# Small tiles shared, odd maxima searched a step ahead, and small maps written in halves, in a two-layer convolution and attention kernel

## The chip, the cores and the metric

The kernel runs on one core of a Trainium2 chip. The metric is the device time of one execution in microseconds (us). The engines are TensorE (PE, with its weight loads shown apart as PEld), VectorE (DVE), ScalarE (ACT), GpSimd (POOL) and SyncE (SP), which here only issues DMAs. All data are 32-bit floats.

## The reference

The input x has 8 images of 256 channels and 64 x 64 pixels. Two layers follow each other, each added to its input after a group norm `_gn` over 32 groups of channels.

```python
# layer 0, on n = _gn(x)
x1, x2, x3 = conv1x1(n, w1, b1), conv1x1(n, w2, b2), conv1x1(n, w3, b3)   # 32, 32, 256 maps
h = relu(bn1(concat([x1, unfold3(pad(x2, "reflect"))])))                  # 32 + 9 * 32 maps
w = conv1x1(relu(bn2(conv1x1(h, cw1))), cw2, cb2)      # 9 weights for each of 32 groups
x = x + einsum("bgskhw,bgkhw->bgshw", unfold3(pad(x3)), w)

# layer 1, on n = _gn(x)
q, k, v = conv1x1(n, Wq, bq) * HD**-0.5, conv1x1(n, Wk, bk), conv1x1(n, Wv, bv)   # 4 heads of 64
att = softmax(q . (unfold7(pad(k, "reflect")) + unfold7(pad(pe, "reflect"))))     # 49 neighbours
out_att = sum over neighbours of att * unfold7(pad(v, "reflect"))
wts = softmax over 9 of conv1x1(n, Wfc)                # 9 maps for each channel
out_conv = sum over 9 of depthwise(relu(depthwise(n, w1)), w2) * wts
x = x + rate1 * out_att + rate2 * out_conv
```

## The kernel before

An image is cut into 8 bands of 8 rows. The main loop runs over g from -12 to 63. For g at or above 0 it does layer 1 of band i = g % 8 of image b = g // 8, and beside it layer 0 of the band that lies 12 ahead (AHEAD), so layer 0 ends at g = 51. For g below 0 only layer 0 runs ("alone"). A band has 8 steps: s = 0 to 3 for the first 128 channels, 4 to 7 for the others. m = s % 4 is the step within a half, and a step covers two tiles of 8 x 8 queries. An image's first and last bands (i = 0 and 7) have another order of queries and keys than the six between.

The order of the work is the order in which Python issues it: each engine runs its instructions in that order. A step consists of fixed parts with six calls of `advance()` between them. `after(n, f)` puts f off by n such calls (six are one step), so that an instruction is issued when its operands should be there. `beside(g, s)` returns three lists of extra work for a step: `head` (issued before the exponentials), `mid` (in the middle) and `end`. `steer(g, s)` issues loads and starts the statistics. What a function in `mid` returns is called one `advance()` later.

PSUM has eight banks here: four with the tag "gen", two for scores ("sco"), one "small", one "acc". "gen" serves the results of most matmuls: `pf` (branch weights, L883), `p3` (value maps of layer 0, L373; the trace calls them p), `pq` and `pk` (queries L681, keys L703), `pv` (values, L598), `ptp` (transposed probabilities, L784), `pw` (tap weights, L468), and the group means `pg` (L242), biases `pb` (L308) and channel means `pgc` (L546). A bank is handed on when the instruction that reads it has run: ACT's exponential L888 for pf, its copies L786, L378 and L605 for ptp, p3 and pv, DVE's products L481 for pw.

The "small" bank has one buffer, a new one for each even step. It holds the weighted values of two steps (256 columns, matmuls L796, added to xr by DVE at L815), and in part of the steps, beside them, the small maps of layer 0 (p12, columns 256 to 511 at s = 0, L332) or the 32 hidden maps (columns 256 to 383 at s = 4 and 6, L432).

A step in layer 1: at even m, PE makes the scores of two steps (L747) and the weighted values of earlier ones. `masked` (DVE, L761) searches the maxima of one step, `exponentials` (ACT, L769) follows, `probabilities` takes a reciprocal on DVE (L776) and scales on ACT (L778). `branch_weights` runs twice a step: four matmuls into pf and an exponential into ex; POOL adds ex (L1099). `depthwise_begin` and `depthwise_middle` give taps on DVE (L840, L866), two at a time. `keys` ends in four DVE instructions a piece (L711, L718) that write the key block kb with its mirrored columns. `dynamic_sum` divides by the sum of the exponentials (L896 to L910, with DVE's reciprocals L904).

Layer 0 beside it: `small_maps` (four matmuls, each in several instructions) and `write_maps`, eight ACT copies (L347, L351) into x2 and four POOL copies for its edges (L355 to L364); `value_maps`; `hidden_maps` (ACT L422); `tap_weights` with products on DVE (L481) that POOL adds to xg (L489).

Statistics: `gn_affine` runs a1 to a6, spread by `after`: two group means on PE (k = 0 and 1), DVE arithmetic between (a2 reads the first, L251 to L255; a4 the second, L263), ACT for the root (L146), DVE for the biases (L273). It is used by `scaled_weights` (at i = 3 for the next image of layer 0, ending in `through` and `biases`, L316) and by `norm_rows` (at i = 6 for the next image of layer 1, ending in `by_channel` and `take`, L551), both from step 2.

Values: `values` makes them in two halves, ACT copies them to vc (L605), `store_values` writes vc to DRAM (L618, L622), `mirror_rows` mirrors rows there (L629), `value_tile` loads them as vt (L640). `position` makes the position term pe on POOL for the first image and keeps it in DRAM (L661, on SP's queue). Those that `beside` moves:

```python
if s == 3 and not early:
    mid.append(lambda: keys(b, i, 1))
...
made = [(b + 1, 0, (3, 4)), (b + 1, 1, (5, 7))]
...
if s in d and (j < NB or s == d[0]):
    mid.append(lambda bb=bb, j=j, d=d: values(bb, j, d.index(s)))
if s == d[1]:
    end.append(lambda bb=bb, j=j: store_values(bb, j))
```

Of the kernel before, what the change touches and what calls it, by code (L numbers as in the profile page):

```python
# [10 lines left out]
F32 = mybir.dt.float32  # L11
# [7 lines left out]
P = 128  # L19
C = 256  # L20
NCT = C // P
H = W = 64
HW = H * W
R = 8
# [63 lines left out]
def conv_layers_kernel(ctx: ExitStack, tc: tile.TileContext, ins: dict, out: bass.AP):  # L88
# [131 lines left out]
    def after(n, f):  # L220
        later.append((place[0] + n, f))

    def advance():
# [3 lines left out]
        for f in ready:  # L227
            f()

    def gn_affine(sts, means, name, done):  # L230


        n = len(sts)
        mv = stat.tile([P, n, 2], F32, name=f"mv_{name}", tag=f"mv{n}")
        for ct, st in enumerate(sts):
            nc.vector.bn_aggr(mv[:, ct, :], st)
        mean, var = mv[:, :, 0], mv[:, :, 1]
        gm, d, sc, bi = (stat.tile([P, n], F32, name=f"{v}_{name}", tag=f"{v}{n}") for v in ("gm", "d", "sc", "bi"))

        def group_means(v, k):  # L240
            pg = ps.tile([P, n], F32, name=f"pg_{name}_{k}", tag="gen", bufs=4)
            nc.tensor.matmul(pg, means, v, start=True, stop=True)  # L242
            return pg


        def a1():
            pg = group_means(mean, 0)
            after(2, lambda: a2(pg))

        def a2(pg):  # L250
            nc.vector.tensor_copy(gm, pg)  # L251
            for ct in range(n):
                c = slice(ct, ct + 1)
                nc.vector.tensor_scalar(d[:, c], pg[:, c], mean[:, c], None, ALU.subtract)
                nc.vector.tensor_scalar(d[:, c], d[:, c], d[:, c], var[:, c], ALU.mult, ALU.add)  # L255
            after(5, a3)

        def a3():
            pg = group_means(d, 1)
            after(2, lambda: a4(pg))  # L260

        def a4(pg):
            nc.vector.tensor_scalar(sc, pg, GN_EPS, None, ALU.add)  # L263
            after(2, a5)

        def a5():
            inverse_root(sc)
            after(4, a6)

        def a6():  # L270
            for ct in range(n):
                c = slice(ct, ct + 1)
                nc.vector.tensor_scalar(bi[:, c], gm[:, c], sc[:, c], -1.0, ALU.mult, ALU.mult)  # L273
            done(sc, bi)

        after(3, a1)
# [15 lines left out]
    def scaled_weights(b):  # L292

        im = images[b]

        def scale(sc, bi):
            im.w12s = w0.tile([P, NCT, 2 * REL], F32, tag="w12s", name=f"w12s_{b}", bufs=1)
            im.w3s = w0.tile([P, NCT, C], F32, tag="w3s", name=f"w3s_{b}", bufs=1)
            for kt in range(NCT):
                nc.scalar.activation(im.w12s[:, kt], w12[:, kt], AF.Copy, scale=sc[:, kt : kt + 1])  # L300
                nc.scalar.activation(im.w3s[:, kt], w3[:, kt], AF.Copy, scale=sc[:, kt : kt + 1])
            after(5, lambda: through(bi))

        def through(bi):
            pb = ps.tile([P, 1 + NCT], F32, tag="gen", name=f"pb_{b}", bufs=4)
            for m, to, w in ((0, 0, w12), (0, 64, w12), (1, 0, w3[:, :, :P]), (2, 0, w3[:, :, P:])):
                for kt in range(NCT):
                    nc.tensor.matmul(  # L308
                        pb[to : to + w.shape[2], m : m + 1], w[:, kt], bi[:, kt : kt + 1],
                        start=(kt == 0), stop=(kt == NCT - 1),  # L310
                    )
            after(2, lambda: biases(pb))

        def biases(pb):
            im.bias = w0.tile([P, 1 + NCT], F32, tag="bias", name=f"bias_{b}")
            nc.vector.tensor_add(im.bias[:, 0:1], pb[:, 0:1], par[:, PB21 : PB21 + 1])  # L316
            for ct in range(NCT):
                nc.vector.tensor_add(
                    im.bias[:, 1 + ct : 2 + ct], pb[:, 1 + ct : 2 + ct], chan[:, ct, CB3 : CB3 + 1]
                )  # L320

        gn_affine([im.st0[:, ct] for ct in range(NCT)], gmat, f"a{b}", scale)

    def small_maps(b, i, home):


        im = images[b]

        p12 = home[:, 2 * P :].rearrange("p (r c) -> p r c", r=R // 2)
        for kt in range(NCT):  # L330
            for u in range(2):
                nc.tensor.matmul(  # L332
                    p12[64 * u : 64 * u + 64], im.w12s[:, kt, :],
                    im.xc[i][:, kt, u * BAND // 2 : (u + 1) * BAND // 2],
                    start=(kt == 0), stop=(kt == NCT - 1),
                )
        return lambda: write_maps(b, i, p12)

    def write_maps(b, i, p12):
        im = images[b]  # L340
        t = im.x2[i] = w0.tile([P, HR, W], F32, tag="x2", name=f"x2_{b}_{i}", bufs=2)
        bias = im.bias
        for u in range(2):
            r, o = u * R // 2, 64 * u
            for q, (dst, src) in enumerate(((1, 0), (0, 0), (0, 1))):
                n = W - (q != 1)
                nc.scalar.activation(  # L347
                    t[32 * q : 32 * q + 32, r + 1 : r + 1 + R // 2, dst : dst + n],
                    p12[o : o + 32, :, src : src + n], AF.Identity, bias=bias[o : o + 32, 0:1],
                )  # L350
            nc.scalar.activation(  # L351
                t[96:128, r : r + R // 2, :], p12[o + 32 : o + 64], AF.Identity, bias=bias[o + 32 : o + 64, 0:1]
            )

        nc.gpsimd.tensor_copy(t[0:32, 1 : 1 + R, 0:1], t[0:32, 1 : 1 + R, 2:3])  # L355
        nc.gpsimd.tensor_copy(t[64:96, 1 : 1 + R, W - 1 : W], t[64:96, 1 : 1 + R, W - 3 : W - 2])

        if i == 0:
            nc.gpsimd.tensor_copy(t[0:96, 0, :], t[0:96, 2, :])
        else:  # L360
            nc.gpsimd.tensor_copy(t[0:96, 0, :], im.x2[i - 1][0:96, R, :])
            nc.gpsimd.tensor_copy(im.x2[i - 1][0:96, R + 1, :], t[0:96, 1, :])
        if i == NB - 1:
            nc.gpsimd.tensor_copy(t[0:96, R + 1, :], t[0:96, R - 1, :])  # L364
# [168 lines left out]
    def norm_rows(b):  # L533
# [7 lines left out]
            after(3, lambda: by_channel(both))  # L541

        def by_channel(both):
            pg = ps.tile([P, NCT, 2], F32, tag="gen", name=f"pgc_{b}", bufs=4)
            for ct in range(NCT):
                nc.tensor.matmul(pg[:, ct], gc[:, ct], both, start=True, stop=True)  # L546
            after(2, lambda: take(pg))
# [35 lines left out]
    def values(b, j, half):  # L583
# [2 lines left out]

        im = images[b]
        if half == 0:
            im.vc[j] = w1.tile([P, R // 2, C], F32, tag="vc", name=f"vc_{b}_{j}", bufs=1)
        vc, yp = im.vc[j], im.yp[min(j, NB - 1)]  # L590
        first, last, _ = value_rows(j)
        pv = ps.tile([P, 2, C], F32, tag="gen", name=f"pv_{b}_{j}_{half}", bufs=4)
# [54 lines left out]
    def position(b, i):  # L647
# [10 lines left out]
            perow[:, a : a + n].unsqueeze(2).to_broadcast([P, n, W]),  # L658
        )
        kept[i] = dram.tile([P, n, W], F32, tag=f"pe{i}", name=f"pe_{i}", bufs=1)  # L660
        nc.sync.dma_start(out=kept[i], in_=pe[:, :n])  # L661

    kept = {}

# [259 lines left out]
    def beside(g, s):  # L924
# [6 lines left out]
        if g >= 0:  # L931
            if s == 2:
                mid.append(lambda: keys(b, i, 1) if early else queries(b, i, 1))
            if s == 3 and early:
                head.append(lambda: queries(b, i, 1))
            if s == 3 and not early:
                mid.append(lambda: keys(b, i, 1))
        edge = inx in (0, NB - 1)
        if 0 <= g + 1 < B * NB:
            if s == 5 - edge:  # L940
# [5 lines left out]

        made = [(b, i + 2, (4, 5))] if g >= 0 and i < NB - 1 else []
        if i == NB - 1 and 0 <= b + 1 < B:
            made = [(b + 1, 0, (3, 4)), (b + 1, 1, (5, 7))]
        for bb, j, d in made:  # L950
            if s in d and (j < NB or s == d[0]):
                mid.append(lambda bb=bb, j=j, d=d: values(bb, j, d.index(s)))
# [21 lines left out]
        if 0 <= g + AHEAD < B * NB:  # L974
            bq_, iq = divmod(g + AHEAD, NB)
            if alone and s == 0:
                mid.append(lambda: small_maps(bq_, iq, small_tile(f"{bq_}_{iq}"))())
            if s == (2 if alone else 0):
                (mid if alone else end).append(lambda: value_maps(bq_, iq, 0, alone))
            if s == (3 if alone else 1):  # L980
# [40 lines left out]
    with tc.manual_schedule():  # L1021
# [17 lines left out]
        for n, f in enumerate(layer1_loads()):  # L1039
            after(4 * STEPS * (3 + n), f)  # L1040

        pending, before, conv, convs = [], None, None, []
        for g in range(-AHEAD, B * NB):
            b, i = divmod(g, NB)
            for s in range(STEPS):
                ct, m = divmod(s, NT // 2)
                head, mid, end = beside(g, s)
                steer(g, s)
                if g >= 0:
                    nm = f"{b}_{i}_{ct}_{m}"  # L1050
                    weighted = []
                    if m % 2 == 0:
                        sco = score_tile(nm)
                        for e in range(2):
                            scores(b, i, ct, m + e, sco)
                        small = small_tile(nm)
                        weighted, pending = weigh_steps(pending, small), []
                        if s == 0 and g + AHEAD < B * NB:
                            mid.append(small_maps(*divmod(g + AHEAD, NB), small))
                        if s in (4, 6) and convs:  # L1060
                            convs.pop()(small)
                        if before is not None:
                            pending.append((before[:-1], transposed(nm, before[-1])))
                    prob, nmax = masked(nm, m, sco)
                    for a, po in weighted:
                        add_values(*a, po)
                ahead = [f() for f in head]
# [41 lines left out]
                advance()  # L1109
                for f in end:  # L1110
                    f()
                advance()
        for last in (before, None):
            for a, po in weigh_steps(pending, small_tile(f"end{last is None}")):
# [88 lines left out]
```

## Time and profile before

| What | Before |
|---|---|
| median of 3 runs | 3902.41 us (3900.53 to 3902.47) |
| profiled execution | 3901.4 us |
| its span | 3899.5 us |
| PE, DVE, ACT, POOL busy | 97%, 88%, 72%, 80% of the span |
| layer 0 alone, up to band 0's scores | 233.5 us |
| a band between two starts of scores, i = 1, 2, 4, 5 | 57.5 to 57.6 us in most |
| the same, i = 3, 6, 7, 0 | 60.4, 57.5, 61.2, 59.5 us in most |
| bands without layer 0 (g = 56 to 62) | 47.2 to 49.6 us |

The span runs from the first instruction of the program to the last; the execution's own time is 1.9 us longer. A timeline row gives start and length in us, engine, line, operation, what is written and read, a count of merged instructions, and in brackets the idle time before and who ended it. A row of waits gives who waited for whom, the total in us, how often, and the longest. The granted PE clock was 0.994 of full over the span, and 1.00 in every stretch that I read from 300 us to 3800 us.

### The profile page before, as it was taken

Reading aid. Unit: us, or ns where it says so; the run is one execution under the profiler, and the core shown is the slowest. Engines: PE = TensorE matmul, PEld = TensorE weight load, DVE = VectorE, ACT = ScalarE, POOL = GpSimd, SP = SyncE. Lnnn points to the kernel's source line nnn. Section 1 sums busy time; section 2 is a strip of 40 time slices with the busy share of each in tenths; the row PEclk is TensorE's granted clock in tenths of the full one; section 3 lists DMA queues with packets and bytes.
Section 4 is the critical chain, followed back from the end, with each engine's and each line's share of the span. In section 5 each row is a group of like instructions: output and inputs, shape, how many; then the busy total and the mean of one; then the engine's idle time right before and its main releaser. Section 6 shows DMA issues by size and latency. Waiting matters only on the chain.

```text
span 3899.5 us, 71759 instructions
## 1 busy us (share of the span) xinstructions
PE 3774.0 (97%) x24620; PEld 2112.0 (54%) x24620; DVE 3415.8 (88%) x7125; ACT 2809.8 (72%) x6770; POOL 3118.1 (80%) x2100
## 2 busy tenths in 40 slices
PE   6889999999999999999999999999999999999998
PEld 3445555555555555555555555555555555555554
DVE  6879999889988989899998998989988889978777
ACT  4457777777777777777777777777777777677776
POOL 4768888888987988888888888978988888955665
PEclk9999999999999999999999999999999999999999
DMA  8754544544544543544544544454543543332221
GB/s 247 211 162 128 142 113 126 155 124 113 136 127 131 148 120 104 151 137 118 145 112 136 143 124 116 132 145 119 139 113 102 145 123 101 89 94 81 78 66 37
DMA packets 438926, 490.14 MB, mean 126 GB/s; under 512 B 62016, under 2 KB 324256, under 8 KB 438304
## 3 DMA queue, kind: packets, MB, share of 16 engines
q1 hardware_dynamic: 421984, 469.79, 43.4%
q10 hardware_dynamic: 16576, 15.76, 1.3%
q8 instruction: 194, 3.18, 0.3%
q14 instruction: 172, 1.41, 0.1%
HBM read 343.76 MB, written 145.10 MB: 125 GB/s over the span
## 4 chain that ended last, share of the span: by engine, by line
PE 38%; POOL 22%; DVE 20%; ACT 10%; issue 5%; DMA 4%; SPq 0%; ACTq 0%; POOLq 0%; DVEq 0%
PE pf L883 18%; POOL xg L489 10%; POOL ex L1099 7%; DVE prod L481 6%; DVE rec L904 4%; DVE acc L866 4%; PE small L796 3%; ACT x L347 3%; PE pv L598 3%; PE ptp L784 3%; PE sco L747 3%; PE pq L681 2%; PE pk L703 2%; DMA x<-x3n 2%; ACT ex L888 2%
## 5 line engine op out<-in xcount | busy, mean ns | idle before, releaser
L883 PE MATMUL pf<-yp,c_wfc 128*128 128x512 f32 x4096 | 1916.3, 594 | 16.7 <-ACT ex L888 10.3
L489 POOL TENSOR_TENSOR xg<-xg,prod 128x1024 f32<-128x1024 f32 x549 | 1201.0, 2188 | 108.7 <-DVE prod L481 82.7
L883 PEld LDWEIGHTS pf<-yp,c_wfc 128*128 128x128 f32 x4096 | 738.6, 190 | 715.7 <-issue 628.4
L1099 POOL TENSOR_TENSOR ex<-ex,ex 128x1024 f32<-128x1024 f32 x384 | 908.2, 2365 | 68.7 <-ACT ex L888 65.2
L840 DVE SCALAR_TENSOR_TENSOR acc<-yp,c_chan,acc 128x504 f32<-128x504 f32 (+3 forms) x1104 | 775.8, 703 | 63.3 <-ACT acc L831 42.9
L481 DVE SCALAR_TENSOR_TENSOR prod<-pw,c_par,x3q 128x1040 f32<-128x1040 f32 x576 | 737.3, 1287 | 92.3 <-PE pw L468 47.8
L866 DVE SCALAR_TENSOR_TENSOR acc<-hid,c_chan,acc 128x504 f32<-128x504 f32 (+3 forms) x1024 | 751.5, 734 | 18.1
L888 ACT ACTIVATE ex<-pf 128x512 f32<-128x512 f32 x1024 | 602.3, 588 | 220.7 <-PE pf L883 204.4
L769 ACT ACTIVATE prob<-prob,nmax 128x196 f32<-128x196 f32 x1024 | 459.2, 451 | 205.2 <-DVE nmax L761 204.9
L778 ACT ACTIVATE prob<-prob,tot 128x196 f32<-128x196 f32 x1024 | 413.0, 452 | 262.0 <-DVE tot L776 259.9
L905 POOL TENSOR_TENSOR tot<-tot,rec 128x256 f32<-128x256 f32 x254 | 185.7, 731 | 413.4 <-DVE rec L904 407.3
L904 DVE RECIPROCAL rec<-tot 128x256 f32<-128x256 f32 x256 | 445.8, 1741 | 8.2 <-POOL tot L899 6.6
L786 ACT COPY pt<-ptp 112x512 f32<-112x512 f32 x511 | 295.0, 577 | 111.3 <-PE ptp L784 110.8
L761 DVE CUSTOM_DVE_ANT_0 prob<-sco,c_mask 128x196 f32<-128x196 f32 x1024 | 324.8, 355 | 27.1 <-PE sco L747 27.0
L784 PEld LDWEIGHTS ptp<-ident,prob 128*112 128x112 f32 x2044 | 227.3, 133 | 184.8 <-issue 154.7
L784 PE MATMUL ptp<-ident,prob 128*112 128x128 f32 x2044 | 319.5, 279 | 0.2 <-ACT vc L605 0.2
L796 PEld LDWEIGHTS small<-pt,vt 112*64 112x64 f32 x8144 | 258.5, 138 | 83.5 <-issue 75.4
L796 PE MATMUL small<-pt,vt 112*64 112x64 f32 x8144 | 294.1, 225 | 7.2 <-DMA vt<-vd 7.2
L373 PE MATMUL p<-xc,w3s 128*128 128x512 f32 x512 | 248.1, 608 | 12.6 <-ACT ex L888 12.6
L598 PE MATMUL pv<-c_wv,yp 128*128 128x256 f32 x1056 | 252.3, 381 | 1.7 <-ACT yp L570 1.7
L899 POOL TENSOR_SCALAR tot<-tot 128x512 f32<-128x512 f32 x127 | 243.6, 1918 | 11.1
L468 PEld LDWEIGHTS pw<-h2n,c_c 128*128 128x128 f32 x1152 | 176.1, 192 | 138.2 <-issue 122.3
(136 smaller groups left out, 4655.4 us busy)
## 6 DMA issues: line engine op xcount, KB each, us to landing
vt<-vd SPq DMA_DIRECT2D x512, 112.0 KB
x3q<-x SPq DMA_DIRECT2D x128, 264.0 KB
xc<-in_x SPq DMA_DIRECT2D x64, 512.0 KB
xg<-in_xg SPq DMA_DIRECT2D x64, 512.0 KB
yp<-x SPq DMA_DIRECT2D x128, 256.0 KB
xr<-x SPq DMA_DIRECT2D x64, 512.0 KB
out_x<-xr SPq DMA_DIRECT2D x64, 512.0 KB
xs<-in_x SPq DMA_DIRECT2D x57, 512.0 KB
```

What stands on the lines that cost most here:

```text
L481: nc.vector.scalar_tensor_tensor(prod[:, :, :RUN], pw[:, j, :RUN].unsqueeze(1).to_broadcast([P, SHARE, RUN]), par[:, PCB2 + k : PCB2 + k + 1],
L489: nc.gpsimd.tensor_add(im.xg[i], im.xg[i], rows(prod))
L769: nc.scalar.activation(prob[:, h, :NKEY], prob[:, h, :NKEY], AF.Exp, bias=nmax[:, h : h + 1], scale=-1.0, accum_out=tot[:, h : h + 1],)
L778: nc.scalar.activation(prob[:, h, :NKEY], prob[:, h, :NKEY], AF.Copy, scale=tot[:, h : h + 1])
L784: nc.tensor.transpose(ptp[:, h, ch], prob[:, h, ch * CHUNK : (ch + 1) * CHUNK], ident)
L796: nc.tensor.matmul(po[half[h], :, t * TQ : (t + 1) * TQ], im.vt[i + ch, m][:n, t, (2 * ct + h) * HD : (2 * ct + h + 1) * HD], pt[:n, h, ch ...
L840: nc.vector.scalar_tensor_tensor(o, yp[:, ct, ra + dr : rb + dr, ca + dc : cb + dc], chan[:, ct, CW1 + k : CW1 + k + 1], o, ALU.mult, ALU.add,
L866: nc.vector.scalar_tensor_tensor(o, hid[:, ra + dr : rb + dr, ca + dc : cb + dc], chan[:, ct, CW2 + k : CW2 + k + 1], o, ALU.mult, ALU.add,)
L883: nc.tensor.matmul(pf, wfc[:, kt, 2 * m + j, ct * P : (ct + 1) * P], images[b].yp[i][:, kt, PAD : PAD + R], start=(kt == 0), stop=(kt == N ...
L888: nc.scalar.activation(ex[:, j].rearrange("p (r c) -> p r c", r=R), pf, AF.Exp)
L904: nc.vector.reciprocal(rec, v)
L1099: after(4, lambda ex=ex, exb=exb: nc.gpsimd.tensor_add(ex, ex, exb))
```

## The change

Seven things are edited.

1. Group means, channel means and biases are written to columns 384 and up of the current step's "small" tile, where there is one (`narrow`; not at s = 0 and not before band 0, where they stay in "gen"). Two delays in `gn_affine` become one call shorter each.
2. `write_maps` takes the halves to write; at s = 0 only the first half is written, and the second in `mid` of s = 1, ahead of what else is there, with the edge copies.
3. `masked` of an odd step is issued at the end of the even step before it.
4. At s = 3 of the bands i = 1 to 6, `keys` goes from `mid` to `head`.
5. Ahead of band 0, the second half of band 1's values is made at s = 6 instead of 7, and stored then.
6. Those values use a buffer of the tag "ex" instead of the one buffer "vc".
7. The DMA that keeps pe is issued nine `advance()` calls later.

```diff
+    homes = []
+
+    def narrow(name, at, n):
+
+        if not homes:
+            return ps.tile([P, n], F32, tag="gen", name=name, bufs=4)
+        return homes[0][:, 3 * P + at : 3 * P + at + n]
+
     def gn_affine(sts, means, name, done):
...
         def group_means(v, k):
-            pg = ps.tile([P, n], F32, name=f"pg_{name}_{k}", tag="gen", bufs=4)
+            pg = narrow(f"pg_{name}_{k}", 4 * k, n)
...
-            after(5, a3)
+            after(4, a3)
 
         def a3():
             pg = group_means(d, 1)
-            after(2, lambda: a4(pg))
+            after(1, lambda: a4(pg))
...
         def through(bi):
-            pb = ps.tile([P, 1 + NCT], F32, tag="gen", name=f"pb_{b}", bufs=4)
+            pb = narrow(f"pb_{b}", 8, 1 + NCT)
...
-        return lambda: write_maps(b, i, p12)
-
-    def write_maps(b, i, p12):
-        im = images[b]
-        t = im.x2[i] = w0.tile([P, HR, W], F32, tag="x2", name=f"x2_{b}_{i}", bufs=2)
-        bias = im.bias
-        for u in range(2):
+        im.x2[i] = w0.tile([P, HR, W], F32, tag="x2", name=f"x2_{b}_{i}", bufs=2)
+        return lambda u: write_maps(b, i, p12, u)
+
+    def write_maps(b, i, p12, half):
+        im = images[b]
+        t, bias = im.x2[i], im.bias
+        for u in half:
...
+        if half[-1] == 0:
+            return
...
         def by_channel(both):
-            pg = ps.tile([P, NCT, 2], F32, tag="gen", name=f"pgc_{b}", bufs=4)
+            pg = narrow(f"pgc_{b}", 12, NCT * 2).rearrange("p (t n) -> p t n", t=NCT)
...
         if half == 0:
-            im.vc[j] = w1.tile([P, R // 2, C], F32, tag="vc", name=f"vc_{b}_{j}", bufs=1)
+            tag, bufs = ("ex", 3) if (b, j) == (0, 1) else ("vc", 1)
+            im.vc[j] = w1.tile([P, R // 2, C], F32, tag=tag, name=f"vc_{b}_{j}", bufs=bufs)
...
-        nc.sync.dma_start(out=kept[i], in_=pe[:, :n])
+        after(9, lambda: nc.sync.dma_start(out=kept[i], in_=pe[:, :n]))
...
             if s == 3 and not early:
-                mid.append(lambda: keys(b, i, 1))
+                head.append(lambda: keys(b, i, 1))
...
-            made = [(b + 1, 0, (3, 4)), (b + 1, 1, (5, 7))]
+            made = [(b + 1, 0, (3, 4)), (b + 1, 1, (5, 7 if g >= 0 else 6))]
...
-                mid.append(lambda: small_maps(bq_, iq, small_tile(f"{bq_}_{iq}"))())
+                mid.append(lambda: small_maps(bq_, iq, small_tile(f"{bq_}_{iq}"))((0, 1)))
...
-        pending, before, conv, convs = [], None, None, []
+        pending, before, conv, convs, maps = [], None, None, [], []
...
                 head, mid, end = beside(g, s)
+                if s == 1:
+                    mid, maps = maps + mid, []
...
                         small = small_tile(nm)
+                        homes[:] = [small] if s else []
                         weighted, pending = weigh_steps(pending, small), []
                         if s == 0 and g + AHEAD < B * NB:
-                            mid.append(small_maps(*divmod(g + AHEAD, NB), small))
+                            write = small_maps(*divmod(g + AHEAD, NB), small)
+                            mid.append(lambda write=write: write((0,)))
+                            maps.append(lambda write=write: write((1,)))
...
-                    prob, nmax = masked(nm, m, sco)
+                    prob, nmax = masked(nm, m, sco) if m % 2 == 0 else odd
...
                 for f in end:
                     f()
+                if g >= 0 and m % 2 == 0:
+                    odd = masked(f"{b}_{i}_{ct}_{m + 1}", m + 1, sco)
                 advance()
```

## The prediction

> **What bounds the kernel now.** I read the page first, then TensorE's (PE's) waits, then the timelines of PE, ScalarE (ACT), VectorE (DVE) and SyncE (SP) around each kind of wait. First the page's row of busy times, then the waits of PE: in total, times, longest.
>
> ```profile
> PE 3774.0 (97%) x24620; PEld 2112.0 (54%) x24620; DVE 3415.8 (88%) x7125; ACT 2809.8 (72%) x6770; POOL 3118.1 (80%) x2100
> ```
>
> ```profile
> PE p L373 <- ACT ex L888: 12.6, 52, 0.9
> ...
> PE pf L883 <- ACT ex L888: 10.3, 16, 0.7
> PE small L796 <- DMA vt<-vd: 7.2, 2, 6.7
> PE pf L883 <- DVE prod L481: 6.4, 6, 1.1
> PE pg_a L242 <- ACT ex L888: 5.2, 6, 1.1
> PE sco L747 <- DVE kb L718: 5.2, 29, 0.2
> ```
>
> PE is the bound, and its idle time is a short list of stalls, each recurring at one place of a band. A removed stall is time gained, until another engine is late at the next place. Starts count here, not idle times. In band 29 PE runs transposes (ptp), then the second value map (p):
>
> ```profile
> 1952.55 0.60 PE L784 MATMUL ptp<-ident,prob 128*112 128x128 f32 x4
> 1953.33 1.98 PE L373 MATMUL p<-xc,w3s 128*128 128x512 f32 x4 [0.18 <-ACT ex L888]
> ```
>
> From start to start that is 0.78 us; where the next matmul is ready, four transposes take 0.44 (1967.15 to 1967.59). So the stall is 0.34, and the stalled block itself takes 1.82 us, against 1.72, before the next starts: 0.105 to get going again. ACT shows why:
>
> ```profile
> 1948.85 1.39 ACT L347 ACTIVATE x<-small,bias 32x252 f32<-32x252 f32 x3
> 1950.26 0.47 ACT L351 ACTIVATE x<-small,bias 32x256 f32<-32x256 f32 x1
> 1950.73 1.43 ACT L347 ACTIVATE x<-small,bias 32x252 f32<-32x252 f32 x3
> 1952.19 0.47 ACT L351 ACTIVATE x<-small,bias 32x256 f32<-32x256 f32 x1
> 1952.68 0.60 ACT L888 ACTIVATE ex<-pf 128x512 f32<-128x512 f32 x1
> ```
>
> Eight copies of the small maps (3.83 us) stand ahead of the exponential that frees the "gen" bank which p needs. I measured every place so, from 228 us on. The stalls, restart included: p after transposes 52 times, 26.5; scores on key padding 29 times, 7.2; group means (L242) on ACT 12 times, 9.1; the channel means of norm_rows (L546) 6 times, 4.3; pf on a product 6 times (i=7, step 6), 8.3; pf after values 8 times (step 5), 6.8; queries at i=0 6 times, 3.0; pf after keys in bands 52 and 53, 1.7. With small restarts some 74 us, and one wait of 6.67 us on a DMA at the start. After band 53 there is nothing to speak of.
>
> **What the skill says.** "Perfetto Trace Analysis", Tensor Engine Instruction: a matmul's reported end is an estimate. The trace agrees (0.18 idle reported, 0.34 by starts). "PSUM — Partial Sum Buffer", Engine vs sequencer instructions: ACT, DVE and POOL are strict FIFO; agrees, as the exponential above sits behind copies that it doesn't need. The same page, PSUM bank collisions: guard a bank by bank and quadrant, not by address, so columns beside the weighted values are not free of their bank's other users. The trace agrees: DVE's xr L815 waits 18.2 us in all for small L332, which writes other columns.
>
> **Small maps in halves.** No instruction is added; four of eight ACT copies (L347, L351) move from step 0 to step 1, and four POOL edge copies with them. In band 29 ACT then ends the first half at 1950.73, the exponential at 1951.3, x3n at 1951.9; the maxima are there at 1950.92, so the exponentials of step 1 end at 1952.8, not 1954.8; then ex, pt copy and scaling to 1954.4, second half to 1956.3, x3n to 1957.0, ex to 1957.5 (before: 1957.6). PE needs the freed bank at 1953.0: 1.7 us to spare. All of this stall goes: **-26.5**. The cost: the copies must be out of the one-buffer "small" bank before the weighted values of step 2 (before at 1958.26, now 0.45 earlier, 1957.8): 1.5 us to spare, so nothing. POOL's copies wait till 1956.5 with nothing urgent behind (its next, L905, started at 1958.24), and the hidden maps that read them begin on ACT at 1959.7.
>
> DVE gains too: its reciprocal waited 2.54 us for step 1's exponentials; free 1.9 us sooner, it is next held by pw of PE, so I take DVE as 1.0 us earlier through steps 2 and 3.
>
> **Keys ahead (step 3).** The same four matmuls stand before pf and transposes, and DVE's four key operations (1.08 us) before four taps. They then end near 1969.1 in band 29, and scores want them near 1971: -7.2. The bank order becomes that of i=7, where queries stand at that place and nothing stalls. In bands 52 and 53 the pf after keys goes with it: **-8.9** together.
>
> **Maxima of odd steps ahead.** No instruction more; two searches (0.64 us) pass one product of 1.29 us. Before, in an i=0 band at step 5, DVE ran the product at 2159.51 and the search ended at 2161.36; the exponential that frees PE's bank ended at 2162.58, PE having been ready at 2161.69. 1.2 us from the order and 1.0 from above put that end at 2160.4: this stall goes, **-6.8**. The product passed is 0.64 later, but the second product's end, which frees pw, is unchanged.
>
> **Means and biases beside.** The matmuls stay (restarts too), only their bank changes. The channel means need no gen bank and their reader on DVE (L551) is over 1 us ahead of the next step 6: **-4.3**. For the group means I expect a new wait instead. In band 27:
>
> ```profile
> 1849.65 1.88 PE L703 MATMUL pk<-yp,c_wk 128*128 128x512 f32 x4
> 1852.61 0.38 PE L242 MATMUL pg_a<-d_a,c_gmat 128*128 128x2 f32 x2 [1.08 <-ACT ex L888]
> ```
>
> ```profile
> 1856.50 0.15 DVE L263 TENSOR_SCALAR sc_a<-pg_a 128x2 f32<-128x2 f32 x1
> ```
>
> Now L263 reads from "small", and step 4's weighted values (L796, before at 1856.13) can't write there until it has. The same DVE work stands ahead of it, so it ends near 1856.65 - 1.1 = 1855.55; PE, without 0.45 and 1.08 of stalls, arrives at 1854.6. A wait of about 1.0 takes the place of 1.08; in band 30 I get 0.55 for 0.6. Behind L796 stand PE's transposes, pf and values. So **0**, between -9 (DVE in time) and +6. Biases (three DVE adds, behind L904) come about when step 6 arrives: 0, at most 0.5 x 6.
>
> **The rest.** pf on a product at i=7 is POOL's: the product waited 0.51 for a buffer, POOL being dense from 2076 to 2106. It starts about 1 us earlier, PE some 0.5: **-3**, between 0 and -8. Queries at i=0: pq needs the exponential just behind it; 0.
>
> **First values.** SP before:
>
> ```profile
> 224.64 0.32 SPq L661 DMA_DIRECT2D pe<-pe  x1
> ...
> 246.59 1.33 SPq L618 DMA_DIRECT2D vd<-vc  x2
> 247.97 4.07 SPq L622 DMA_DIRECT2D vd<-vc  x6
> 252.75 3.12 SPq L640 DMA_DIRECT2D vt<-vd  x4
> ```
>
> ```profile
> 255.78 0.70 PE L796 MATMUL small<-pt,vt 112*64 112x64 f32 x8 [6.67 <-DMA vt<-vd]
> ```
>
> SP idled from 207.6 until POOL made pe at 224.6, with the first values (on ACT at 220.7) behind. Moved nine places on, L661 lets them go at 220.8; the second values' own "ex" buffer spares ACT its 8.99 us wait, and their stores go a step earlier. Adding SP's issues from 220.8 (4.6 stores, 4.1 xr and x3q, 0.4 pe, 1.9 mirrors, 5.4 stores, 0.5, 4.0, 5.6, 3.1) gives 250.4, landing near 251.5; PE resumes there, not at 255.8: **-4.3**, between 0 (another wait for scores or yp) and -9. No DMA is added.
>
> **The sum.** -26.5 - 8.9 - 6.8 - 4.3 + 0 - 3 - 4.3 = -53.8. I take off 4 for restarts and small new waits: **-50**. The profiled execution took 3901.4 us (span 3899.5), 1.0 under the median of 3902.41, so the forecast against the median is 3852. 0.2% (7.8 us) is about what a measurement of this kernel can tell from no change.
>
> **Rivals.** *A: only maps and keys pay* (chance 0.2). DVE (88% busy) and POOL stay late at steps 4 to 6, so the waits there and the start keep their size: -26.5 - 8.9 = -35, less a few: 3870. For it: the product stall is POOL's. Against: DVE's own longest wait in a band is the one that the halves shorten. *B: nearly all stalls go* (0.1): -74 - 7 = 3822. Against: group means now wait for a DVE that is behind. *C: "small" is the new bound* (0.07): step 2's weighted values wait for ACT's second half in each of 52 bands. Gains of 50 are about 1 us a band, the margin is 1.5: the change turns slower when the second half ends over 2.5 us later than I place it, for instance with ACT held by a late reciprocal; at 3.0 us that is +0.5 x 52 = +26, 3928. Against: ACT has no wait over 0.5 us in step 1 of the bands I read. *D: no effect* (0.03): the gen banks are handed out in another order and each stall moves to the next bank.
>
> **How the numbers follow.** Main case 0.6, A 0.2, B 0.1, C 0.07, D 0.03. Main: 3852, its own range 3838 to 3866. The range goes to 3832 and 3882, taking in A and half of the way to B, with the ends of the unknown costs. Faster 0.89, within 0.2% 0.04, slower 0.07.
>
> **What would show it.** Right: p L373 on ACT gone from PE's waits; a typical band of 56.9 us between starts, where it was 57.57; scores on kb L718 gone; L242 and L546 no longer waiting on ACT; a wait of small L796 on DVE sc L263 of 0.5 to 1 us, 12 times; the first vt wait under 6 us and ended near 251. Wrong: L796 waiting on ACT x L347 or L351 in every band (C), or pk and pf waiting on ACT instead of p (D).

## The result, and the profile after

| | Before | After |
|---|---|---|
| median | 3901.8 us (4 runs) | 3859.1 us (3857.7 to 3860.7, 4 runs) |
| ratio | 1 | 0.9891, 95% interval 0.9874 to 0.9908 |
| profiled execution, its span | 3901.4, 3899.5 us | 3859.1, 3856.5 us |
| band 0's first scores | 233.5 us | 235.3 us |
| band 1's first scores | 301.6 us | 298.4 us |
| from there to the end of the span | 3597.9 us | 3558.1 us |

42.7 us less than before, where 50 less had been forecast (3852, range 3832 to 3882). The span of the profiled execution is 43.0 shorter: 39.8 of that lies behind the start of band 1 and 3.2 ahead of it.

The page's row of busy times first: PE does the same 24620 instructions, and the share that it is busy reads 97% as before. That row doesn't show the gain.

```profile
PE 3758.0 (97%) x24620; PEld 2111.3 (55%) x24620; DVE 3434.6 (89%) x7125; ACT 2809.4 (73%) x6770; POOL 3116.9 (81%) x2100
```

The waits of PE show it (total, times, longest; L796 is now L807, L242 L250, L263 L271, L883 L894, L888 L899):

```profile
PE pf L894 <- DVE prod L491: 6.4, 6, 1.1
PE small L807 <- DVE sc_a L271: 5.7, 6, 1.0
PE pf L894 <- ACT ex L899: 4.5, 16, 1.0
PE small L807 <- DVE sc_b L271: 3.0, 6, 0.5
...
PE pw L478 <- ACT ex L899: 1.8, 1, 1.8
PE small L807 <- ACT x L359: 1.5, 1, 1.5
```

Gone are the 52 waits of p for ACT, the 29 of scores for kb, and the 12 of group means for ACT. New are 12 waits of the weighted values for DVE's reading of a group mean. The product's 6 waits stand unchanged. The last row, the weighted values waiting for ACT's copies, is one wait, in band 0.

Band 29 again, now the step-1 stretch, PE and then ACT:

```profile
1927.42 0.60 PE L795 MATMUL ptp<-ident,prob 128*112 128x128 f32 x4
1927.86 1.88 PE L383 MATMUL p<-xc,w3s 128*128 128x512 f32 x4
```

```profile
1925.13 0.47 ACT L359 ACTIVATE x<-small,bias 32x256 f32<-32x256 f32 x1
1925.62 0.60 ACT L899 ACTIVATE ex<-pf 128x512 f32<-128x512 f32 x1
...
1930.94 0.47 ACT L359 ACTIVATE x<-small,bias 32x256 f32<-32x256 f32 x1
```

Four transposes take 0.44 from start to start; p follows at once. The exponential that p needs ends at 1926.2, and the second half of the copies at 1931.4, 1.3 us before the weighted values (1932.69) write their bank.

### The profile page after: what moved, and what is told of

It reads as the page before. It is cut to its first block, busy times and chain, and to the rows that moved or that the text cites. A ratio compares the mean times of both kernels' runs of the same rounds, so it can differ in the third digit from the quotient of the medians.

```text
span 3856.5 us, 71633 instructions
## 1 busy us (share of the span) xinstructions
PE 3758.0 (97%) x24620; PEld 2111.3 (55%) x24620; DVE 3434.6 (89%) x7125; ACT 2809.4 (73%) x6770; POOL 3116.9 (81%) x2100
## 4 chain that ended last, share of the span: by engine, by line
PE 79%; DVE 8%; POOL 7%; ACT 2%; DMA 2%; issue 1%; SPq 0%; ACTq 0%; POOLq 0%; DVEq 0%
PE pf L894 38%; PE small L807 6%; PE ptp L795 6%; PE pv L609 5%; PE pk L714 5%; PE p L383 5%; PE pq L692 5%; PE sco L758 5%; POOL xg L499 4%; DVE prod L491 3%; PE pw L478 2%; DVE acc L877 2%; POOL ex L1115 2%; PE small L340 1%; PE small L442 1%
## 5 line engine op out<-in xcount | busy, mean ns | idle before, releaser
L894 PE MATMUL pf<-yp,c_wfc 128*128 128x512 f32 x4096 | 1918.0, 594 | 10.8 <-DVE prod L491 6.4
L894 PEld LDWEIGHTS pf<-yp,c_wfc 128*128 128x128 f32 x4096 | 739.3, 190 | 710.1 <-issue 654.5
L899 ACT ACTIVATE ex<-pf 128x512 f32<-128x512 f32 x1024 | 603.8, 590 | 358.4 <-PE pf L894 286.0
L807 PEld LDWEIGHTS small<-pt,vt 112*64 112x64 f32 x8144 | 258.6, 138 | 88.6 <-issue 56.7
L807 PE MATMUL small<-pt,vt 112*64 112x64 f32 x8144 | 294.2, 225 | 11.3 <-DVE sc_a L271 5.7
```

The lines of the kernel that those rows point to most:

```text
L807: nc.tensor.matmul(po[half[h], :, t * TQ : (t + 1) * TQ], im.vt[i + ch, m][:n, t, (2 * ct + h) * HD : (2 * ct + h + 1) * HD], pt[:n, h, ch ...
L894: nc.tensor.matmul(pf, wfc[:, kt, 2 * m + j, ct * P : (ct + 1) * P], images[b].yp[i][:, kt, PAD : PAD + R], start=(kt == 0), stop=(kt == N ...
L899: nc.scalar.activation(ex[:, j].rearrange("p (r c) -> p r c", r=R), pf, AF.Exp)
```

## The experiments

How they are read. Two executions of one kernel differ by some 2 us (up to 8 over 13 runs). Two kernels were profiled twice, and there the profiles say where. The changed kernel started band 0 at 235.3 and 233.3, and its times were 3859.1 and 3857.0; from band 1's scores to the end it took 3558.1 and 3558.3. The kernel channel_early (below) took 3853.1 and 3851.3, and 3552.5 and 3552.9 of it from band 1 on. So in these pairs the scatter lies ahead of band 1, mostly in the stretch of layer 0 alone. There the granted PE clock differs too: over all profiles it is 0.87 to 0.95 between 150 and 230 us, and 1.00 in each from 300 to 3800 us. Whether the clock makes the scatter, no run tells. So beside the median and its ratio to the kernel before on the same chip, the table has **the stretch from band 1's first scores to the end**, which repeats within 0.4 us in these pairs, and the median distance between the starts of two bands, which repeats within 0.02. Columns i = 0 to 7 give that distance for bands that have layer 0 beside them; a difference of the stretch under some 0.5 us is not read as one. What an edit is worth "in company" is the changed kernel less the changed kernel without this edit.

| Kernel | median | ratio (95%) | band 1 starts | band 1 to end | i=0 | i=1 | i=3 | i=6 | i=7 |
|---|---|---|---|---|---|---|---|---|---|
| before | 3901.8 | 1 | 301.6 | 3597.9 | 59.53 | 57.58 | 60.36 | 57.46 | 61.22 |
| maps_only | 3865.5 | 0.9901 (0.9886 to 0.9916) | 304.5 | 3560.7 | 58.89 | 56.86 | 59.46 | 56.56 | 60.75 |
| keys_only | 3900.6 | 0.9997 (0.9988 to 1.0005) | 303.1 | 3597.1 | 59.52 | 57.57 | 60.27 | 57.37 | 61.27 |
| odd_only | 3900.3 | 0.9991 (0.9983 to 0.9999) | 299.0 | 3594.2 | 58.82 | 57.58 | 60.37 | 57.41 | 61.29 |
| after | 3859.1 | 0.9891 (0.9874 to 0.9908) | 298.4 | 3558.1 | 58.13 | 56.85 | 60.10 | 56.31 | 60.77 |
| no_odd | 3864.0 | 0.9900 (0.9885 to 0.9915) | 299.1 | 3563.4 | 58.89 | 56.86 | 60.20 | 56.30 | 60.75 |
| no_keys | 3856.8 | 0.9885 (0.9870 to 0.9900) | 295.6 | 3556.8 | 58.12 | 56.85 | 60.02 | 56.23 | 60.76 |
| no_start | 3860.4 | 0.9895 (0.9880 to 0.9910) | 301.1 | 3557.9 | 58.12 | 56.85 | 60.10 | 56.30 | 60.76 |
| no_means | 3854.3 | 0.9872 (0.9855 to 0.9888) | 297.5 | 3556.1 | 58.16 | 56.86 | 59.56 | 56.47 | 60.76 |
| channel_means | 3865.9 | 0.9905 (0.9890 to 0.9920) | 295.8 | 3566.9 | 58.17 | 56.86 | 59.56 | 58.04 | 60.76 |
| channel_early | 3851.3 | 0.9869 (0.9854 to 0.9884) | 298.7 | 3552.5 | 58.11 | 56.86 | 59.56 | 55.96 | 60.75 |
| values_late | 3844.0 | 0.9851 (0.9837 to 0.9864) | 294.5 | 3545.1 | 58.12 | 56.86 | 59.55 | 55.96 | 59.45 |

### The halves alone (maps_only)

```diff
 (to the kernel before)
-        for u in range(2):
+        for u in half:
...
+                            mid.append(lambda write=write: write((0,)))
+                            maps.append(lambda write=write: write((1,)))
```

> The kernel before with the small maps in halves alone. Theory (each stall is worth what it measured, and they add up): the stall of p on ACT goes, -26.5, and nothing else: 3901.8 - 26.5 = 3875. Rival 1 (DVE, freed about 1 us a band, also ends the stalls of step 5 and of the group means): -26.5 - 6.8 - 9 = about 3860. Rival 2 (the stall goes on to pw or to the next gen bank): under half is gained, 3888 or more.

Measured: 37.2 less from band 1 on, between theory and rival 1, closer to the latter. The bands of i = 1 lost 0.72, which is about the stall of p with its restart (0.45) and the wait for padded keys (0.24) together. Of 29 waits for kb two are left. Why, DVE's waits say, the kernel before and then the halves alone:

```profile
DVE tot L776 <- ACT prob L769: 164.1, 78, 3.9
```

```profile
DVE prod L483 <- PE pw L470: 88.2, 97, 2.4
DVE tot L778 <- ACT prob L771: 67.8, 88, 3.1
```

The reciprocal of step 1 no longer waits for an ACT behind eight copies. In band 29 the key instructions on DVE start 0.73 us earlier after the band's first scores (27.36 for 28.09), while PE has gained 0.45; the 0.28 between them is more than the 0.24 that the scores of step 4 had waited for kb. Part of what DVE won it gives back in waiting for PE (47.8 us before on that row, 88.2 now). In bands of i = 3, 0.90 went: besides 0.45 of p, half of the group means' wait. One edit did the work of two.

### The keys ahead: alone, and taken out of the whole (keys_only, no_keys)

```diff
 (to the kernel before; no_keys reverses it in the changed one)
-                mid.append(lambda: keys(b, i, 1))
+                head.append(lambda: keys(b, i, 1))
```

> The kernel before with the keys of step 3 moved ahead, alone. Theory (an edit is worth its stall only where nothing else has taken the stall away): scores no longer wait for padded keys, -7.2, p still waits for ACT in 52 bands: 3902 - 7 = 3895. Rival (the gen banks are handed out in another order and the stall moves to the next bank, or p's stall grows): 3900 or more.

> The changed kernel with the keys of step 3 where they were, behind pf and the transposes; all other edits stay. Theory (overlap: with the halves alone scores waited for padded keys 2 times and not 29, 0.6 us for 7.2, so the halves already did what this edit is for): 3859 to 3861, no difference. Rival (each part earns its own sum of the prediction): 3859 + 8.9 = 3868.

Measured: alone 0.8 from band 1 on, and no clear difference in the medians: the rival. Taken out of the whole, the kernel was 1.3 shorter there: no gain in company either, as the theory of overlap had it. That theory holds for the bands i = 1, 2, 4 and 5, where scores don't wait for kb without the edit. In the six bands of i = 3 they do, 0.66 us each, but the wait of L807 on L271 behind them is then 0.50 and not 0.95 (in the view the total is 3.0 for 5.7): there too the stall changes places, and the band takes 60.02 for 60.10. In no_keys (the two other waits of this row are those of bands 52 and 53):

```profile
PE sco L758 <- DVE kb L729: 6.4, 8, 1.2
```

Alone, scores wait for kb nowhere any more, and a band still takes 57.57. Where the 0.24 goes is seen later, at step 5, in band 29 with its keys ahead:

```profile
1983.33 1.89 PE L598 MATMUL pv<-c_wv,yp 128*128 128x256 f32 x8
1985.23 1.98 PE L883 MATMUL pf<-yp,c_wfc 128*128 128x512 f32 x4
1987.05 0.39 PE L468 MATMUL pw<-h2n,c_c 128*128 128x132 f32 x2
```

```profile
1982.57 1.89 PE L598 MATMUL pv<-c_wv,yp 128*128 128x256 f32 x8
1984.30 1.91 PE L883 MATMUL pf<-yp,c_wfc 128*128 128x512 f32 x4
1986.04 0.39 PE L468 MATMUL pw<-h2n,c_c 128*128 128x132 f32 x2
```

(The second fence is the kernel before.) Band 29's first scores start at 1943.41 and 1942.40. Measured from there, pv starts 0.25 sooner with the keys ahead (39.92 for 40.17). From pv to pf it then takes 1.90 instead of 1.73, pf itself 1.82 instead of 1.74, and pw starts at 43.64 in both. ACT's exponential that frees pf's bank, again with the keys ahead and then before:

```profile
1984.58 0.60 ACT L888 ACTIVATE ex<-pf 128x512 f32<-128x512 f32 x1 [0.53 <-POOL ex L1099]
```

```profile
1983.57 0.60 ACT L888 ACTIVATE ex<-pf 128x512 f32<-128x512 f32 x1 [0.28 <-POOL ex L1099]
```

It ends 41.77 after the first scores in both: it waited for POOL, which nothing had moved. The view of waits has "PE pf L883 <- ACT ex L888: 10.3, 16, 0.7" in both kernels: a stall of 0.17 can't be told there, only from start to start.

### The maxima of odd steps: alone, and taken out (odd_only, no_odd)

```diff
 (to the kernel before; no_odd reverses it in the changed one)
-                    prob, nmax = masked(nm, m, sco)
+                    prob, nmax = masked(nm, m, sco) if m % 2 == 0 else odd
...
+                if g >= 0 and m % 2 == 0:
+                    odd = masked(f"{b}_{i}_{ct}_{m + 1}", m + 1, sco)
```

> The kernel before with the odd steps' maxima searched in the step ahead, alone. Theory of overlap (in company the edit was worth 5.3, the stall of pf after values at step 5; p still waits for ACT's copies in 52 bands): -5 to -9: 3893 to 3897. Rival 1 (an earlier DVE cures the other short waits too, as with the halves): 3885 or less. Rival 2 (the stall moves on, as with the keys alone): 3900 or more.

> The changed kernel with the odd steps' maxima searched in their own step, as before; all other edits stay. Theory: pf after values at step 5 waits again (6.8 less what the halves give), and DVE is later at L271, so that the wait of L807 on it grows by 0.3 to 0.6 in 12 places: 3859 + 6.8 + 5 = about 3870. Rival (the halves alone make the exponentials early enough; the order of maxima is worth nothing): 3859.

Measured: alone 3.7, in company 5.3, nearly all of it in the bands of i = 0 (0.71 and 0.76 a band): the pf behind values at step 5. Alone it was less than expected, and by the medians alone (2.1 less, ratio 0.9983 to 0.9999) it would hardly be told from nothing. In the bands of i = 3 and 6 the group means no longer waited for ACT, but nothing was gained, as these waits of PE show:

```profile
PE sco L747 <- DVE kb L718: 13.0, 35, 1.2
...
PE pf L883 <- ACT ex L888: 4.4, 7, 0.7
PE sco L747 <- POOL xg L489: 4.0, 6, 0.7
```

Of 16 waits of pf for ACT 7 are left, and the six of i = 0 are gone. There are six more waits for kb, all at i = 3 and of 0.98 us each, and six for POOL at i = 6, of 0.67 each: the stall moved on. (The rest of the first row's growth is bands 52 and 53, where the wait for kb rises from 0.24 to 1.2 without any change of the bands' time.) Out of the whole, the odd maxima left the wait of L807 on L271 as it was (5.3 and 3.0 us by the view), so the theory's second term, +5, was wrong.

### Means and biases: all back, or some (no_means, channel_means, channel_early)

```diff
 no_means (to the changed kernel)
-                        homes[:] = [small] if s else []
+                        homes[:] = []
-            after(4, a3)
+            after(5, a3)
-            after(1, lambda: a4(pg))
+            after(2, lambda: a4(pg))
```

> The changed kernel with group means, channel means and biases back in gen banks at their old distances; all other edits stay. Theory (the odd maxima already make ACT's exponentials early enough, so the move to small only added the waits of L807 on L271, 9.7, and of pf on ex behind them, 4.0): those 13.7 go, the channel means cost at most their 4.3 again: 3859 - 13.7 + (0 to 4.3) = 3845 to 3850. Rival (the prediction's account: the old waits of L250 and L556 on ACT come back, 9.1 and 4.3, for the 13.7): 3859, no difference.

channel_means instead puts only pg and pb back into gen banks, at the old distances:

```diff
 channel_means (to the changed kernel; after(5, a3) and after(2, ...a4) as above)
-            pg = narrow(f"pg_{name}_{k}", 4 * k, n)
+            pg = ps.tile([P, n], F32, tag="gen", name=f"pg_{name}_{k}", bufs=4)
-            pb = narrow(f"pb_{b}", 8, 1 + NCT)
+            pb = ps.tile([P, 1 + NCT], F32, tag="gen", name=f"pb_{b}", bufs=4)
```

> The changed kernel with group means and biases back in gen banks at their old distances, the channel means of norm_rows still beside the weighted values. Theory: as no_means, less what the channel means would wait in a gen bank there (0 to 4.3): 3845. If it equals no_means, then the odd maxima cure the channel means too, and the whole of part 1 earns nothing. Rival (old waits come back for the group means): 3859.

Measured: no_means 2.0 less than the change, not 9 to 14; channel_means 8.8 more. No expectation gave the latter. First the group means in the changed kernel, band 27:

```profile
1826.99 0.28 PE L250 MATMUL small<-d_a,c_gmat 128*128 128x2 f32 x2
1827.47 1.98 PE L894 MATMUL pf<-yp,c_wfc 128*128 128x512 f32 x4 [0.19 <-ACT ex L899]
...
1831.70 1.15 PE L807 MATMUL small<-pt,vt 112*64 112x64 f32 x32 [0.95 <-DVE sc_a L271]
```

```profile
1830.05 1.54 DVE L877 SCALAR_TENSOR_TENSOR acc<-hid,c_chan,acc 128x512 f32<-128x512 f32 x2
1831.49 0.15 DVE L271 TENSOR_SCALAR sc_a<-small 128x2 f32<-128x2 f32 x1
```

L807 stood ready at 1830.75 and could write once L271, in DVE's queue behind taps, had read. In a gen bank (no_means) that wait doesn't exist, and the old one of 1.08 us for ACT is now 0.3 (the row of pg_b, at i = 6, reads the same):

```profile
PE pg_a L250 <- ACT ex L899: 1.9, 6, 0.3
```

So moving the group means costs 0.54 a band at i = 3 (60.10 for 59.56). The channel means at the old distances are the same mechanism at its worst; band 30 of channel_means, PE and DVE:

```profile
2022.05 1.15 PE L807 MATMUL small<-pt,vt 112*64 112x64 f32 x32 [2.02 <-DVE aff L561]
```

```profile
2020.22 1.75 DVE L915 RECIPROCAL rec<-tot 128x256 f32<-128x256 f32 x1
2021.89 0.10 DVE L561 COPY aff<-small 128x4 f32<-128x4 f32 x1
```

A copy of 0.10 us behind a reciprocal of 1.75 holds the weighted values for 2.02. The changed kernel avoids that only by its two shorter delays, which bring the copy two calls ahead. That gave a candidate: group means and biases in gen banks, channel means beside, and the short delays for the channel statistics alone.

```diff
 channel_early (to channel_means)
-            after(5, a3)
+            after(5 - (n == 1), a3)
-            after(2, lambda: a4(pg))
+            after(2 - (n == 1), lambda: a4(pg))
```

> A candidate: the changed kernel with group means and biases in gen banks and the channel means beside the weighted values, read at the changed kernel's distances (4 and 1 for the channel statistics alone, 5 and 2 for the others). Theory (a value beside the weighted values is free of charge only where its reader on VectorE has ended before PE comes to the bank's next use; at distances 5 and 2 it came 2.0 us late in 6 bands, at 4 and 1 it comes in time): the 12.5 of the kernel with channel means alone go, and the 2.1 of pf behind L556 with them: about 3852. Rival (group means in a gen bank meet another order of banks in bands of i=6): 3859 or more.

Measured: 5.6 less than the change from band 1 on, median 3851.3, as expected. Against no_means the channel means beside are worth 3.6, together with the two shorter delays of the channel statistics; the short delays with all means in gen banks were not tried. Against the change, the group means and biases back in gen banks are worth 5.6, with the old delays at i = 3.

### The start (no_start)

```diff
 (to the changed kernel)
-            tag, bufs = ("ex", 3) if (b, j) == (0, 1) else ("vc", 1)
-        after(9, lambda: nc.sync.dma_start(out=kept[i], in_=pe[:, :n]))
+        nc.sync.dma_start(out=kept[i], in_=pe[:, :n])
-            made = [(b + 1, 0, (3, 4)), (b + 1, 1, (5, 7 if g >= 0 else 6))]
+            made = [(b + 1, 0, (3, 4)), (b + 1, 1, (5, 7))]
```

> The changed kernel with the three edits of the start undone (second values in their own buffer, their distance, the write of pe). Theory: the 6.7 us wait for vt in band 0 comes back for the 1.0 us wait for vt, the 1.8 us of pw on ex and the 1.6 us of L807 on x: band 0 is longer by 5, scores begin up to 1.8 sooner: 3859 + 3 to 5 = 3862 to 3864. Rival (the prediction's lower bound: those other waits are there in any case): 3859.

Measured: behind band 1 no difference (3557.9), and band 0 itself took 68.6 us against 63.1 with the edits. Its start scatters, so the medians can't settle a size. Over all profiles the five without the edits took 67.5 to 68.6 for band 0 and the nine with them 62.8 to 64.1: about 5 us. In the changed kernel PE went on from its wait for vt 19.3 us after band 0's first scores (22.3 before; 18.0 had been forecast). The wait itself shrank from 6.67 to 1.00, and pw's wait of 1.81 on an exponential came in part instead (0.7 us from start to start without the edits, 2.0 with them): SP now issues xs at 241.46 (236.11 in the kernel before), behind the early stores, and DVE stood 5.74 us for it. That this is what delays the exponential was read from the trace, not tried.

### Two candidates beside the change

values_late follows from the wait that no edit had touched, pf on the product at i = 7. The prediction gave it to POOL. But PE may be asking for that bank sooner there than elsewhere: bands of i = 7 make values of the next image at steps 3, 4, 5 and 7.

```diff
 values_late (to channel_early)
-            made = [(b + 1, 0, (3, 4)), (b + 1, 1, (5, 7 if g >= 0 else 6))]
+            made = [(b + 1, 0, (3, 4)), (b + 1, 1, (6, 7) if g >= 0 else (5, 6))]
```

> The changed kernel once more, beside the two candidates on one chip: 3859 again, ratio 0.989 to the kernel before.

> The candidate with group means in gen banks and the channel means beside, once more, beside the changed kernel on one chip. Theory (its stalls sum to 29.7 against 38.1, so 8.4 less): 6 to 10 below the changed kernel. Rival (the 8 between the two medians was the chip's or the start's scatter of some 4 us): under 4 below.

> The candidate, and in bands of i=7 the first half of the next image's second values made in step 6 and not in step 5. Theory (pf of step 6 waits there for the last product because the values of step 5 have used up one more gen bank): with them a step later pf takes a bank that an exponential freed, -7.5: some 3844. Rival (POOL is late there, so the wait goes to pv or to the next pf): as the candidate or slower, 3851 or more.

Measured on one chip: the change 3857.5, channel_early 3854.5 (ratio 0.9877, 0.9864 to 0.9891), values_late **3844.0**. From band 1 on: 3558.3, 3552.9, 3545.1. By the medians channel_early alone is 3.0 below the change, which is its rival's forecast and within the scatter of the start; by the stretch it is 5.4, below the 6 to 10 expected. values_late is 13.5 below the change, and the step-6 stall is gone. Channel_early and then values_late, band 31:

```profile
2072.96 0.65 PE L795 MATMUL ptp<-ident,prob 128*112 128x128 f32 x4
2074.66 1.99 PE L894 MATMUL pf<-yp,c_wfc 128*128 128x512 f32 x4 [1.05 <-DVE prod L491]
```

```profile
2063.31 0.65 PE L795 MATMUL ptp<-ident,prob 128*112 128x128 f32 x4
2063.80 1.88 PE L894 MATMUL pf<-yp,c_wfc 128*128 128x512 f32 x4
...
2065.36 1.30 DVE L491 SCALAR_TENSOR_TENSOR prod<-pw,c_par,x3q 128x1040 f32<-128x1040 f32 x1 [0.50 <-POOL xg L499]
```

The product still waits 0.50 for POOL and ends as late as ever, 47.4 us after the band's first scores in both, and PE has passed long since: this pf now starts 1.56 us before the product does, so it no longer depends on it. Of the order of gen tiles only the values' place has changed. That pf now gets another bank follows from this; the views don't name the banks, and which tile held which was not worked out.

## Why the prediction was right, point by point

The direction, the order of size and the main mechanism (ACT's copies out of the way of p) held; that each listed stall is worth its measured length did not. From band 1 on the measured parts, each alone, sum to -37.2 - 0.8 - 3.7, and part 1 in company costs 2.0: -39.7, where -39.8 was measured. With what keys and odd maxima were worth in company (+1.3 and -5.3) the sum is -39.2. That the whole came within 7 of the forecast is in part luck: the halves gave 10.7 more than forecast, and keys, group means, product and odd maxima together some 20 less. The terms of the prediction's sum stand so:

- **Halves: -26.5 forecast, -37.2 measured alone.** The placing in band 29 was right: ACT's second half ended 14.1 us after the band's first scores (forecast 13.9). The stall of p went in full. Mis-sized was the term for this edit, since it priced the stall of p alone. The earlier DVE was forecast (1.0 us through steps 2 and 3) and came (in band 29, 1.0 at step 2 and 0.7 at the keys), but that it would by itself end the waits for the keys in the bands i = 1, 2, 4 and 5 and half of the group means' wait was not priced. Taking the halves out of the whole wasn't tried.
- **Keys: -8.9 forecast, -0.8 measured alone, +1.3 in company.** The step that failed is counting the 7.2, measured as a stall, as a gain. Alone, an exponential took the 0.24 back at step 5; in company the halves had already removed it, but for the bands of i = 3, where it changed places with the wait for L271. The 1.7 of bands 52 and 53 didn't come either: bands 52 to 62 took 553.1 to 553.2 us in every kernel.
- **Odd maxima: -6.8 forecast, -5.3 in company, -3.7 alone.** The place was right.
- **Group means and biases: 0 forecast, +5.6 measured.** The new wait came just as forecast (0.95 against 1.0). It shows what it costs in this program to guard a bank as a whole and not by address, the rule that the prediction took from the Trainium skill ("PSUM — Partial Sum Buffer", PSUM bank collisions): a reader of other columns held the bank's next writer for 0.95 us, and for 2.02 in channel_means. No run here shows what would happen without that guard. What failed was the other side of the comparison: the old wait of 1.08, which it was to replace, would have shrunk to 0.3 by the other edits alone. The prediction had given its own range, -9 to +6, and the value is near its upper end.
- **Channel means: -4.3 forecast, -3.6 measured** (with the shorter delays, as above), and only so; at the old distance they cost 10.8 more than in a gen bank.
- **The product at i = 7: -3 forecast, 0 measured.** The step that failed is its cause. POOL makes the product late; that PE must wait for it is due to the place of the values among the gen tiles. values_late shows it: with the product as late as before, the wait is gone.
- **The start: -4.3 forecast, about -5 in band 0.** The profile of the change shows 3.2 at the start of band 1, since layer 0 alone ended 1.8 later there, within the scatter. The wait for vt ended at 254.55, not near 251: counted from the first scores it gave 3.0 of the 5 (22.3 to 19.3, with 18.0 forecast). The rest came later in band 0, and where is not shown; that the size was met is in part luck.

The 4 taken off for new waits fell short by 7. Rival A, that only maps and keys pay (3870), is not what happened: the odd maxima and the start paid too. But most of the gain is that of the halves, and its sum for maps and keys (-35) is near what the halves alone gave. Rival C, a late second half, had 1.3 us to spare.

## What to carry to other kernels

In this kernel stalls in a list were not gains to be added: one that was removed with the engine behind it still late returned at the next place, and when that engine came early, several went at once. So measure each edit alone and taken out of the whole, over a stretch that leaves out the part of the program that scatters. Before a small result is put into a bank that others write, ask where its reader stands in its engine's queue when the bank's next writer arrives, and price the old place as the other edits will leave it.

## What the runs showed of the hardware

I had not expected how exactly a program repeats: the time from band 1 to the end, over 3500 us, agreed within 0.4 us between two executions, in two kernels whose whole times differed by 2. From 300 to 3800 us the granted PE clock was 1.00 in every profile, between 150 and 230 us it was 0.87 to 0.95.
